# An FFT-like convolution kernel: v's row sums and differences move from GpSimd to VectorE, three quarters of v's statistics go to ACT, and a packed 32x32 product becomes a full one

## The chip, the cores and the metric

The kernel runs on one core of one Trainium2 chip. The metric is the device time of one execution in microseconds (us), the median of three runs. The engines are TensorE (PE, with its weight loads PEld), VectorE (DVE), ScalarE (ACT), GpSimd (POOL) and SyncE (SP), which here only issues transfers. Each of them takes its own instructions in order and waits for others by semaphores.

## The reference, cut to what matters

Sixteen images of sixteen channels, 256x256, float32, go through two layers with a skip connection each. The first is a group norm and a 3x3 circular convolution (written with FFTs). The second is a group norm and a Laplace neural operator: a forward transform, a mixing of channels per frequency (the steady part x1), and a sum of damped exponentials (the transient part x2).

```python
def _L1_conv_ref(x, ty, tx, weights_pole1, weights_pole2, weights_residue):
    ...
    alpha = jnp.fft.fft2(x, axes=(-2, -1))
    ...
    output_residue1 = jnp.einsum('biox,oxik->bkox', alpha, S)
    ...
    output_residue2 = jnp.einsum('bikpq,ikpq->bkpq', D, weights_residue)
    x1 = jnp.fft.ifft2(output_residue1, s=(Ny, Nx), axes=(-2, -1)).real
    ...
    E1 = jnp.exp(weights_pole1[..., None] * tyc)
    E2 = jnp.exp(weights_pole2[..., None] * txc)
    F = jnp.einsum('kbpq,bipz->kbiqz', output_residue2, E1)
    x2 = jnp.einsum('kbiqz,biqx->kizx', F, E2).real
    return x1 + x2 / Nx / Ny

# --- layer 0 (conv_preact) ---
x = x + _L0_conv_ref(_gn(x), L0_conv_weight)
# --- layer 1 (conv_preact) ---
x = x + _L1_conv_ref(_gn(x), L1_conv_ty, L1_conv_tx, ...)
```

Below, v is the result of the first layer. The group norm of the second needs v's mean and variance per group, and the transforms need the sums and differences of rows y and 255 - y of v.

## The kernel before

Everything is float32. There are four stretches in time: the convolution with v's statistics (during which small tables for the operator are also set up), the forward transforms, the mixing, and the inverse transforms with the output.

In the first stretch, `conv(g)` is one step of 387; 24 steps make one image. Each step issues sixteen small products on 32x32 tiles of TensorE. Every six steps, four 128x512 blocks of v (r = 0 to 3) are complete: two (r = 0, 1) belong to rows from the top, two (r = 2, 3), three steps later, to the mirrored rows.

```python
    vp = p1.enter_context(tc.tile_pool(name="vt", bufs=4))
    fp = p1.enter_context(tc.tile_pool(name="v_sums", bufs=2))
    ...
    vst = tp.tile([P, B, 8, 6], FP, name="vst", tag="vst")
    sums = tp.tile([P, 2, B, 8], FP, name="sums", tag="sums")
    ...
        for r in (0, 1) if g % 6 == 5 else (2, 3) if g % 6 == 2 else ():
            ...
            nc.scalar.activation(vt, acc[r], AF.Identity, bias=ready[b][1], **by_sums)
            if r % 2:
                nc.scalar.activation(
                    acc[r], vt, AF.Square, bias=shift[:, b : b + 1], accum_out=sums[:, 1, b, col]
                )
            else:
                later.append((g + 2, vst[:, b, col.start], vt))
            if r == 3:
                lo, hi = acc["v", 0], acc["v", 1]
                both = fp.tile([P, 2, 2, N], FP, name="vsum", tag="vsum")
                nc.gpsimd.tensor_tensor(both, lo, hi, ALU.add)
                nc.gpsimd.tensor_tensor(lo, lo, hi, ALU.subtract)
                folded.append((g + 3, b, u, (both, lo)))
        while later and (later[0][0] <= g or g >= 24 * B + 2):
            _, to, vt = later.pop(0)
            nc.vector.bn_stats(to, vt)
```

So ACT evicts all four blocks from PSUM; for two of them it also sums v and its square (the square goes to PSUM, over the block it came from). VectorE takes statistics of the other two. POOL makes the sum and the difference of the two halves, 128x1024 each, which go to HBM.

The statistics of an image of x come from VectorE and pass through TensorE (`ps_stat`, products with a single column) before its convolution can begin: sixteen `bn_stats`, a `bn_aggr` 24 steps ahead of the image, then operations on one column of `xq`, and the weights `wc`.

```python
        yield 24, lambda: nc.vector.bn_aggr(q[:, 0:2], st)
        ...
        yield 22, lambda: ps.append(spread(g128, mean))
        def about_mean():
            nc.vector.tensor_copy(mu, ps[0])
            nc.vector.tensor_tensor(d, mean, mu, ALU.subtract)
            nc.vector.scalar_tensor_tensor(e, d, d, pvar, ALU.mult, ALU.add)
        yield 21, about_mean
        yield 18, lambda: ps.append(spread(g128, e))
```

The table setup (`make_hat`, `make_c`, `make_exps`, `make_coef`) is spread over the same steps; it uses all engines, POOL among them. `make_exps` writes the exponentials to HBM:

```python
            nc.gpsimd.tensor_scalar(rn, th, 1.0 / (2 * PI), turns, ALU.mult, ALU.add)
            ...
            for c in (c1, c2, c3):
                nc.vector.scalar_tensor_tensor(th, rn, -float(c), th, ALU.mult, ALU.add)
            ...
            for o in range(2 - which):
                nc.sync.dma_start(
                    out=eD[which][o, :, 2 * q : 2 * q + 2].rearrange("p i e t -> p i (e t)"),
                    in_=ex,
                )
```

In the last stretch a unit is four images of one output channel k; there are 64. Per image there are four 128x128 products along x (`ps_p`), and four 128x256 products along y (`ps_f`), two for the steady part and two for the transient part. The transient factor along x (`ps_h`) is made for four images at once from 32x32 tiles:

```python
    def transient_x(k, b0):
        ps_h = [pf.tile([P, 2, N], FP, name="ps_h", tag="ps_f")[:, 0] for _ in range(4)]
        for j in range(4):
            for kq in range(4):
                rows = slice(32 * kq, 32 * kq + 32)
                c = 32 * ((kq + j) % 4)
                nc.tensor.matmul(
                    ps_h[j][c : c + 32],
                    lhsT=o2[rows, b0 + j].rearrange("p r m -> p (r m)"),
                    rhs=et[rows, k].rearrange("p e t -> p (e t)"),
                    start=True,
                    stop=True,
                )
        hs = hsp.tile([P, 4, N], FP, name="hs", tag="hs")
        for j in range(4):
            nc.scalar.copy(hs[:, j], ps_h[j])
        return hs
    ...
    def along_y(ey, hs, pt, r):
        ps = pf.tile([P, 2, N], FP, name="ps_f", tag="ps_f")
        for e, tab in ((0, cosY), (1, sinY)):
            nc.tensor.matmul(ps[:, e], lhsT=tab, rhs=pt[:, e], start=True, stop=False)
            nc.tensor.matmul(ps[:, e], lhsT=ey[:, e], rhs=hs, start=False, stop=True)
        ...
    def load_tables(k, eng=nc.gpsimd):
        eng.dma_start(out=et[:, k], in_=eD[1][0, :, k])
        ey = eyp.tile([P, 4, 2, P], FP, name="ey", tag="ey")
        for j in range(4):
            eng.dma_start(out=ey[:, j], in_=turned[P - 32 * j : 2 * P - 32 * j, k])
        return ey
```

Because the four tiles of image j land in output rows turned by 32 j, the table along y is loaded four times, turned likewise. A product written once in float32 shows as two instructions in the trace.

Of the kernel before, what the change touches and what calls it, by code (L numbers as in the profile page):

```python
# [16 lines left out]
B = 16  # L17
C = 16
# [6 lines left out]
def conv_then_laplace_kernel(ctx: ExitStack, tc: tile.TileContext, a: dict, out: bass.AP):  # L25
# [37 lines left out]
    eD = [dp.tile([n, P, C, 2, P], FP, name=f"eD{n}", tag=f"eD{n}") for n in (2, 1)]  # L63
# [37 lines left out]
    fp = p1.enter_context(tc.tile_pool(name="v_sums", bufs=2))  # L101
    sp = p1.enter_context(tc.tile_pool(name="stats", bufs=2))
# [110 lines left out]
    vst = tp.tile([P, B, 8, 6], FP, name="vst", tag="vst")  # L213
    sums = tp.tile([P, 2, B, 8], FP, name="sums", tag="sums")
    shift = tp.tile([P, B], FP, name="shift", tag="shift")

    def conv(g):
# [20 lines left out]
        for r in (0, 1) if g % 6 == 5 else (2, 3) if g % 6 == 2 else ():  # L238
            at = g if r < 2 else g - 3
            if not 0 <= at < 24 * B:  # L240
                continue
            b, u = at // 24, at // 6 % 4
            if r % 2 == 0:
                acc["v", r // 2] = vp.tile([P, 2, 2, N], FP, name="vt", tag="vt")
            vt = acc["v", r // 2][:, r % 2]
            col = slice(2 * u + r // 2, 2 * u + r // 2 + 1)
            by_sums = {"accum_out": sums[:, 0, b, col]} if r % 2 else {}
            nc.scalar.activation(vt, acc[r], AF.Identity, bias=ready[b][1], **by_sums)  # L248
            if r % 2:
                nc.scalar.activation(  # L250
                    acc[r], vt, AF.Square, bias=shift[:, b : b + 1], accum_out=sums[:, 1, b, col]
                )
            else:
                later.append((g + 2, vst[:, b, col.start], vt))
            if r == 3:
                lo, hi = acc["v", 0], acc["v", 1]
                both = fp.tile([P, 2, 2, N], FP, name="vsum", tag="vsum")
                nc.gpsimd.tensor_tensor(both, lo, hi, ALU.add)  # L258
                nc.gpsimd.tensor_tensor(lo, lo, hi, ALU.subtract)
                folded.append((g + 3, b, u, (both, lo)))  # L260
        while later and (later[0][0] <= g or g >= 24 * B + 2):
            _, to, vt = later.pop(0)
            nc.vector.bn_stats(to, vt)
# [16 lines left out]
    def v_stats(b0, b1, bank):  # L280

        bs, nb = slice(b0, b1), b1 - b0
        n = 8.0 * 512
# [13 lines left out]
        tt(mean, m1, m2, ALU.add)  # L297
        ts(mean, mean, 0.5, None, ALU.mult)
        tt(e, v1, v2, ALU.add)
# [5 lines left out]
        for m in (m1, m2):  # L305
            tt(d, m, mu, ALU.subtract)
            tt(d, d, d, ALU.mult)
            tt(e, e, d, ALU.add)
        ts(e, e, 0.5, None, ALU.mult)
# [86 lines left out]
    def make_coef():  # L396
# [3 lines left out]
        nc.sync.dma_start(out=rs, in_=a["res_kq"])  # L400
        u = sw.tile([P, 4, C, 4], FP, name="s_u", tag="s_rn")
# [15 lines left out]
    def make_exps(which):  # L417
# [10 lines left out]
        for q in range(8):  # L428
# [28 lines left out]
            for o in range(2 - which):  # L457
                nc.sync.dma_start(
                    out=eD[which][o, :, 2 * q : 2 * q + 2].rearrange("p i e t -> p i (e t)"),
                    in_=ex,  # L460
                )
# [583 lines left out]
    eyp = pool(p3, "ey", 2)  # L1045
    kp = pool(p3, "e_const")
    up = pool(p3, "ud", 2)
    hp = pool(p3, "pl", 3)
    hsp = pool(p3, "hl", 2)
    qp = pool(p3, "ql", 3)  # L1050
    pp = pool(p3, "p_p", 2, space=PSUM)
    pf = pool(p3, "p_f", 6, space=PSUM)

    et = ep.tile([P, C, 2, P], FP, name="et", tag="et")
    turned = eD[0].rearrange("o p k e t -> (o p) k e t")
    inv = kp.tile([P, 5, P], FP, name="inv", tag="inv")
    nc.gpsimd.dma_start(out=inv, in_=a["inv"])
    cx, sx, nsx, cosY, sinY = (inv[:, j] for j in range(5))
# [11 lines left out]
    def load_tables(k, eng=nc.gpsimd):  # L1070

        eng.dma_start(out=et[:, k], in_=eD[1][0, :, k])
        ey = eyp.tile([P, 4, 2, P], FP, name="ey", tag="ey")
        for j in range(4):
            eng.dma_start(out=ey[:, j], in_=turned[P - 32 * j : 2 * P - 32 * j, k])
        return ey
# [36 lines left out]
    def transient_x(k, b0):  # L1113


        ps_h = [pf.tile([P, 2, N], FP, name="ps_h", tag="ps_f")[:, 0] for _ in range(4)]
        for j in range(4):
            for kq in range(4):
                rows = slice(32 * kq, 32 * kq + 32)
                c = 32 * ((kq + j) % 4)  # L1120
                nc.tensor.matmul(  # L1121
                    ps_h[j][c : c + 32],
                    lhsT=o2[rows, b0 + j].rearrange("p r m -> p (r m)"),
                    rhs=et[rows, k].rearrange("p e t -> p (e t)"),
                    start=True,
                    stop=True,
                )
        hs = hsp.tile([P, 4, N], FP, name="hs", tag="hs")
        for j in range(4):
            nc.scalar.copy(hs[:, j], ps_h[j])  # L1130
        return hs

    def along_x(u):

        ps = pp.tile([P, 4, P], FP, name="ps_p", tag="ps_p")
        for n, (at, tab) in enumerate(((0, cx), (3, sx), (1, nsx), (2, cx))):
            nc.tensor.matmul(ps[:, at], lhsT=u[:, n], rhs=tab, start=True, stop=True)  # L1137
        pt = hp.tile([P, 2, N], FP, name="pt", tag="pt")
        nc.scalar.copy(pt, ps.rearrange("p (e n) x -> p e (n x)", e=2))
        return pt  # L1140

    def along_y(ey, hs, pt, r):

        ps = pf.tile([P, 2, N], FP, name="ps_f", tag="ps_f")
        for e, tab in ((0, cosY), (1, sinY)):
            nc.tensor.matmul(ps[:, e], lhsT=tab, rhs=pt[:, e], start=True, stop=False)  # L1146
            nc.tensor.matmul(ps[:, e], lhsT=ey[:, e], rhs=hs, start=False, stop=True)  # L1147
# [20 lines left out]
    ey = load_tables(0)  # L1168
# [3 lines left out]
    for b0 in range(4, B, 4):  # L1172
        load_images(yk, b0, slice(0, P), nc.sync)
# [190 lines left out]
```

## Time and profile before

The time is 2940.07 us, the median of three runs (2932.43, 2940.07 and 2942.22). The profiled execution has a span of 2938.3 us.

| engine | busy us | share of the span | instructions |
|---|---|---|---|
| PE | 2685.4 | 91% | 39536 |
| PEld | 1975.1 | 67% | 39536 |
| DVE | 1922.6 | 65% | 3508 |
| ACT | 1506.2 | 51% | 2955 |
| POOL | 1228.4 | 42% | 970 |

The costliest groups of instructions that the change touches or neighbours:

| group | count | busy us | mean ns |
|---|---|---|---|
| PE ps_conv, 32x512 on 32x32 tiles | 12288 | 493.7 | 649 |
| ACT vt, eviction of v, 128x512 | 256 | 161.4 | 681 |
| ACT square, 128x512 | 128 | 88.5 | 692 |
| ACT read of the accumulator after the square | 128 | 23.9 | 186 |
| ACT read of the accumulator after the eviction | 128 | 25.8 | 201 |
| DVE statistics of v, 128x512 | 128 | 86.6 | 677 |
| DVE statistics of x, 128x512 | 256 | 161.7 | 678 |
| PE ps_h, 32x256 on 32x32 tiles | 2048 | 59.5 | 385 |
| PE ps_f, 128x256, the two lines | 2048 | 610.6 | 380 |
| PE ps_p, 128x128 | 2048 | 278.1 | 279 |

"Busy" counts the time in which an engine has an instruction under way; matmuls are pipelined, their modelled durations overlap, and a busy TensorE need not be at its peak. Shares over the whole span mix four stretches with different limits, so each part of the change has to be read in its own stretch. A wait is named by the engine and line that ended it.

### The profile page before, as it was taken

What the parts mean: (1) busy time and instruction counts of PE and PEld (TensorE: products, weight loads), DVE (VectorE), ACT (ScalarE), POOL (GpSimd) and SP (SyncE); (2) the same over time, 40 slices, a digit from 0 to 9 for tenths busy, and PEclk for the clock granted to TensorE, in tenths of its full rate; (3) what the DMA queues carried; (4) which work ended last, traced back from release to release, by engine and by line L of the source; (5) the groups of instructions that cost most, each with busy time, mean ns of one, the idle gap of its engine ahead of it and who ended that gap; (6) DMA issues with size and microseconds to landing.
All of it is one profiled execution on the core that took longest, in us unless ns stands there. A gap on an engine that the chain in (4) does not pass through costs nothing.

```text
span 2938.3 us, 92782 instructions
## 1 busy us (share of the span) xinstructions
PE 2685.4 (91%) x39536; PEld 1975.1 (67%) x39536; DVE 1922.6 (65%) x3508; ACT 1506.2 (51%) x2955; POOL 1228.4 (42%) x970
## 2 busy tenths in 40 slices
PE   4878887777799999999699999999979999999998
PEld 2323333334577777777488888888868888888887
DVE  7666676887488888888544444444426676666666
ACT  3445566755566666666245555555534444444443
POOL 3656666775533333333311111111125555545543
PEclk9989988998899999999899999999989999999999
DMA  6545556674546666665466666667679898989895
GB/s 253 207 159 196 202 207 216 223 244 168 195 173 215 215 230 229 229 218 188 165 194 192 190 194 194 190 192 196 193 196 314 285 291 282 293 281 287 286 287 187
DMA packets 477332, 650.61 MB, mean 221 GB/s; under 512 B 49064, under 2 KB 458664, under 8 KB 462968
## 3 DMA queue, kind: packets, MB, share of 16 engines
q1 hardware_dynamic: 472920, 635.37, 66.7%
q8 instruction: 312, 5.11, 0.7%
q10 hardware_dynamic: 3408, 7.34, 0.7%
q0 software_dynamic: 592, 1.97, 0.3%
q14 instruction: 100, 0.82, 0.1%
HBM read 365.09 MB, written 279.45 MB: 219 GB/s over the span
## 4 chain that ended last, share of the span: by engine, by line
PE 54%; DMA 9%; DVE 7%; SPq 2%; issue 1%; POOL 1%; ACT 0%; DVEq 0%; ACTq 0%; POOLq 0%
PE ps_mix L956 15%; PE ps_s L898 8%; PE ps_y L667 8%; PE ps_y L675 7%; DMA yk<-yD 6%; PE ps_x L710 4%; PE ps_p L1137 3%; PE ps_f L1146 3%; PE ps_f L1147 3%; DVE r L1155 2%; DMA out_y<-ol 2%; SPq L1088 1%; PE psd L695 1%; DVE ol L1157 1%; DVE ol L1158 1%; PE ps_h L1121 1%
## 5 line engine op out<-in xcount | busy, mean ns | idle before, releaser
L231 PE MATMUL ps_conv<-xt,wc 32*32 32x512 f32 x12288 | 493.7, 649 | 30.4 <-ACT vt L248 20.3
L1101 POOL TENSOR_TENSOR u<-yk 128x512 f32<-128x512 f32 x256 | 343.9, 1373 | 369.0 <-PE ps_p L1137 252.6
L956 PEld LDWEIGHTS ps_mix<-abd,sg 128*64 128x64 f32 x8192 | 449.5, 138 | 61.5 <-ACT sg L1016 49.8
L956 PE MATMUL ps_mix<-abd,sg 128*64 128x128 f32 x8192 | 480.4, 276 | 9.5 <-ACT yt L1021 9.5
L231 PEld LDWEIGHTS ps_conv<-xt,wc 32*32 32x32 f32 x12288 | 234.0, 107 | 246.0 <-issue 151.6
L683 ACT ACTIVATE t<-ps_y,vmr 128x384 f32<-128x384 f32 x512 | 297.2, 581 | 170.4 <-PE ps_y L675 157.4
L876 POOL TENSOR_TENSOR w<-v,mcol 128x2048 f32<-128x2048 f32 x33 | 119.2, 3614 | 577.3 <-DVE v L873 574.3
L667 PE MATMUL ps_y<-tabE,vq 128*128 128x256 f32 x1024 | 313.0, 387 | 14.9 <-DVE vq L656 13.2
L1021 DVE COPY yt<-ps_mix 128x512 f32<-128x512 f32 x128 | 88.5, 692 | 360.9 <-PE ps_mix L956 225.2
L675 PE MATMUL ps_y<-tabO,vq 128*128 128x256 f32 x1024 | 305.7, 380 | 0.0
L1146 PE MATMUL ps_f<-pt,inv 128*128 128x256 f32 x1024 | 305.7, 380 | 0.0
L1147 PE MATMUL ps_f<-hs,ey 128*128 128x256 f32 x1024 | 304.9, 379 | 0.0
L1137 PEld LDWEIGHTS ps_p<-inv,u 128*128 128x128 f32 x2048 | 265.1, 192 | 49.1 <-issue 25.1
L1021 ACT COPY yt<-ps_mix 128x512 f32<-128x512 f32 x384 | 218.9, 587 | 149.6 <-PE ps_mix L956 86.5
L248 ACT ACTIVATE vt<-ps_conv,xq 128x512 f32<-128x512 f32 x256 | 161.4, 681 | 258.2 <-PE ps_conv L231 141.9
L1137 PE MATMUL ps_p<-inv,u 128*128 128x128 f32 x2048 | 278.1, 279 | 12.6 <-POOL u L1104 12.6
L898 PE MATMUL ps_s<-ct,w 64*32 64x256 f32 x8448 | 262.6, 384 | 18.6 <-POOL w L876 17.9
L1150 DVE TENSOR_TENSOR r<-ps_f,q 128x256 f32<-128x256 f32 x256 | 107.3, 419 | 252.9 <-ACT q L1149 252.9
L1016 ACT COPY sg<-ps_s 128x512 f32<-128x512 f32 x248 | 159.8, 646 | 197.4 <-PE ps_s L898 197.3
L667 PEld LDWEIGHTS ps_y<-tabE,vq 128*128 128x128 f32 x1024 | 189.4, 190 | 91.4 <-ACT q L723 51.2
L1149 ACT COPY q<-ps_f 128x256 f32<-128x256 f32 x256 | 95.3, 372 | 288.5 <-PE ps_f L1147 286.6
L258 POOL TENSOR_TENSOR vsum<-vt 128x1024 f32<-128x1024 f32 x64 | 153.0, 2391 | 194.1 <-ACT vt L248 119.9
(212 smaller groups left out, 4324.5 us busy)
## 6 DMA issues: line engine op xcount, KB each, us to landing
xt<-in_x SPq DMA_DIRECT2D x32, 2322.0 KB, 9.8
abd<-aD SPq DMA_DIRECT2D x512, 128.0 KB, 3.5
yD<-yt SPq DMA_DIRECT2D x512, 128.0 KB, 2.7
vl<-vD SPq DMA_DIRECT2D x256, 256.0 KB, 3.9
out_y<-ol SPq DMA_DIRECT2D x128, 512.0 KB, 9.6
yk<-yD SPq DMA_DIRECT2D x63, 1024.0 KB, 8.6
s<-vD SPq DMA_DIRECT2D x244, 256.0 KB, 6.7
aD<-spec SPq DMA_DIRECT2D x15, 4096.0 KB, 12.4
```

Of the source, the lines that this page charges most:

```text
L231: nc.tensor.matmul(acc[r][32 * c : 32 * c + 32], lhsT=ready[b][0][rows, phase, tap], rhs=halves[b][u // 2][rows, q : q + 5 : 4, 2 - tap : ...
L248: nc.scalar.activation(vt, acc[r], AF.Identity, bias=ready[b][1], **by_sums)
L667: nc.tensor.matmul(ps[:, 0:N], lhsT=vf[:, xo, 0, j], rhs=tabE[:, 0 : i + 2 : i + 1], start=True, stop=False, skip_group_check=True,)
L675: nc.tensor.matmul(ps[:, P : P + N], lhsT=vf[:, xo, 1, j], rhs=tabO[:, i : C + 1 : C - i], start=False, stop=True, skip_group_check=True,)
L683: nc.scalar.activation(t[:, xo, j].rearrange("p l n -> p (l n)"), ps[:, 0:384], AF.Copy, scale=vmr[:, 0, b0 + j, i : i + 1],)
L898: nc.tensor.matmul(ps[odd][32 * iq : 32 * iq + 32, ro], lhsT=w[rows, iq, kk, ro], rhs=ct[rows, iq, kk], start=True, stop=True,)
L956: nc.tensor.matmul(ps[64 * t : 64 * t + 64, j], lhsT=sg[:, f : f + 2].rearrange("p f m -> p (f m)"), rhs=abd[jq][:, :, 2 * t + cc, 2 * jj ...
L1021: (nc.vector.tensor_copy if m == 3 else nc.scalar.copy)(o, src)
L1101: nc.gpsimd.tensor_tensor(u[:, :, j].rearrange("p b (c n) -> p c b n", c=8), in0, in1, o)
L1137: nc.tensor.matmul(ps[:, at], lhsT=u[:, n], rhs=tab, start=True, stop=True)
L1146: nc.tensor.matmul(ps[:, e], lhsT=tab, rhs=pt[:, e], start=True, stop=False)
L1147: nc.tensor.matmul(ps[:, e], lhsT=ey[:, e], rhs=hs, start=False, stop=True)
```

## The change

It does two things. In the first stretch, the sum and the difference of v's halves are made by VectorE, two steps after the eviction, and POOL keeps only table setup. In return VectorE takes statistics of one block in four instead of two; ACT sums three, and writes the squares to a scratch tile in SBUF instead of PSUM. This is for taking the 128x1024 operations from the slower engine. In the last stretch, the packed 32x32 product of the transient factor is replaced by one full product per image: `ob` holds o2 times a block mask, made once, so that the blocks off the diagonal are zero; the tables need no turned copies then. PSUM is divided anew there (3, 2 and 3 buffers instead of 2 and 6). The formulas that combine the two kinds of statistics get the weights 1 and 3, and two more empty steps stand ahead of `make_coef`.

```diff
+    def mirror(g, b, u, lo, hi):
+        both = fp.tile([P, 2, 2, N], FP, name="vsum", tag="vsum")
+        nc.vector.tensor_tensor(both, lo, hi, ALU.add)
+        nc.vector.tensor_tensor(lo, lo, hi, ALU.subtract)
+        folded.append((g + 3, b, u, (both, lo)))
...
-            nc.scalar.activation(vt, acc[r], AF.Identity, bias=ready[b][1], **by_sums)
-            if r % 2:
+            col = slice(3 * u + r - 1, 3 * u + r)
+            by_sums = {"accum_out": sums[:, 0, b, col]} if r else {}
+            nc.scalar.activation(vt[:, r % 2], acc[r], AF.Identity, bias=ready[b][1], **by_sums)
+            if r == 0:
+                later.append((g + 2, lambda b=b, u=u, v=vt[:, 0]: nc.vector.bn_stats(vst[:, b, u], v)))
+            if r % 2 == 0:
+                continue
+            for k in (1,) if r == 1 else (2, 3):
+                col = slice(3 * u + k - 1, 3 * u + k)
+                junk = jp.tile([P, 2, N], FP, name="junk", tag="junk")
                 nc.scalar.activation(
-                    acc[r], vt, AF.Square, bias=shift[:, b : b + 1], accum_out=sums[:, 1, b, col]
+                    junk,
+                    vt[:, k % 2],
+                    AF.Square,
+                    bias=shift[:, b : b + 1],
+                    accum_out=sums[:, 1, b, col],
                 )
-            else:
-                later.append((g + 2, vst[:, b, col.start], vt))
             if r == 3:
-                lo, hi = acc["v", 0], acc["v", 1]
-                both = fp.tile([P, 2, 2, N], FP, name="vsum", tag="vsum")
-                nc.gpsimd.tensor_tensor(both, lo, hi, ALU.add)
-                nc.gpsimd.tensor_tensor(lo, lo, hi, ALU.subtract)
-                folded.append((g + 3, b, u, (both, lo)))
+                later.append((g + 2, lambda g=g, b=b, u=u, lo=acc["v", 0], hi=vt: mirror(g, b, u, lo, hi)))
...
-            for o in range(2 - which):
-                nc.sync.dma_start(
-                    out=eD[which][o, :, 2 * q : 2 * q + 2].rearrange("p i e t -> p i (e t)"),
-                    in_=ex,
-                )
+            nc.sync.dma_start(
+                out=eD[which][:, 2 * q : 2 * q + 2].rearrange("p i e t -> p i (e t)"), in_=ex
+            )
...
-    pp = pool(p3, "p_p", 2, space=PSUM)
-    pf = pool(p3, "p_f", 6, space=PSUM)
+    pp = pool(p3, "p_p", 3, space=PSUM)
+    ph = pool(p3, "p_h", 2, space=PSUM)
+    pf = pool(p3, "p_f", 3, space=PSUM)
...
+    ob = kp.tile([P, B, 2, 64], FP, name="ob", tag="ob")
+    for kq in range(4):
+        nc.vector.tensor_scalar(
+            ob[:, :, :, 16 * kq : 16 * kq + 16], o2, cols[:, 20 + kq : 21 + kq], None, ALU.mult
+        )
...
-        eng.dma_start(out=et[:, k], in_=eD[1][0, :, k])
-        ey = eyp.tile([P, 4, 2, P], FP, name="ey", tag="ey")
-        for j in range(4):
-            eng.dma_start(out=ey[:, j], in_=turned[P - 32 * j : 2 * P - 32 * j, k])
-        return ey
+        for j in (1, 0):
+            eng.dma_start(out=et[:, j, k], in_=eD[j, :, k])
...
-    def transient_x(k, b0):
...
+    def along_x(k, b, u):
+
+        ps_h = ph.tile([P, N], FP, name="ps_h", tag="ps_h")
+        nc.tensor.matmul(
+            ps_h,
+            lhsT=ob[:, b].rearrange("p r m -> p (r m)"),
+            rhs=et[:, 1, k].rearrange("p e t -> p (e t)"),
+            start=True,
+            stop=True,
+        )
```

## The prediction

> **What bounds the kernel now.** I read the page first (engines, slices, costliest groups), then the busy times of four stretches, because the page's shares average over stages with different limits. Columns: length, busy time with instruction count for TensorE (PE), its weight loads (PEld), VectorE (DVE), ScalarE (ACT) and GpSimd (POOL), then granted clock, DMA share, GB/s. The stretches are the convolution with v's statistics, the forward transforms, the mixing, and the inverse transforms with the output.
>
> ```profile
> 0.00:780.00 780.00, 597.04 (x12644) 283.68 (x12644) 530.43 (x841) 424.71 (x882) 486.48 (x320) 0.91 0.59 206
> 780.00:1410.00 630.00, 617.15 (x4100) 443.63 (x4100) 528.16 (x1213) 372.30 (x641) 220.53 (x285) 0.99 0.60 214
> 1410.00:2172.00 762.00, 731.45 (x16680) 610.99 (x16680) 357.89 (x751) 387.00 (x668) 140.80 (x46) 0.98 0.66 188
> 2172.00:2939.00 767.00, 739.76 (x6112) 636.80 (x6112) 506.14 (x704) 322.19 (x764) 380.62 (x320) 0.99 0.87 276
> ```
>
> Three stretches have TensorE busy 96 to 98% at almost full clock. The first is different: nothing is above 77% (TensorE, and that at a mean clock of 0.91), VectorE 68%, POOL 62%, ACT 54%. The change touches the first and the fourth.
>
> For the fourth I read its TensorE timeline. Columns: start, duration, engine, line, operation, tiles, count.
>
> ```profile
> 2518.86 0.59 PE L1147 MATMUL ps_f<-hs,ey 128*128 128x256 f32 x2
> 2519.38 0.81 PE L1121 MATMUL ps_h<-et,o 32*32 32x256 f32 x32
> 2520.13 1.16 PE L1137 MATMUL ps_p<-inv,u 128*128 128x128 f32 x8
> 2521.12 0.60 PE L1146 MATMUL ps_f<-pt,inv 128*128 128x256 f32 x2
> 2521.55 0.59 PE L1147 MATMUL ps_f<-hs,ey 128*128 128x256 f32 x2
> 2521.99 0.59 PE L1146 MATMUL ps_f<-pt,inv 128*128 128x256 f32 x2
> 2522.42 0.59 PE L1147 MATMUL ps_f<-hs,ey 128*128 128x256 f32 x2
> 2522.85 1.05 PE L1137 MATMUL ps_p<-inv,u 128*128 128x128 f32 x8
> ...
> 2530.80 0.81 PE L1121 MATMUL ps_h<-et,o 32*32 32x256 f32 x32
> ```
>
> Durations overlap, so starts are what to read. One full 128x256 product (two instructions) costs 21.99 - 21.55 = 0.43 us. Between the second and third products along x (2522.85 and 2525.47) an image takes 2.62 us. A unit of four images begins at each ps_h group: 2530.80 - 2519.38 = 11.42 us, of which the packed ps_h group is 11.42 - 4 x 2.62 = 0.94 us. One unit in four is longer, about 12.26 us, as the starts of all 64 groups show; the mean of 62 units after the start is 11.62, so the packed group costs 1.14 us a unit on average. TensorE follows itself without a gap here: the stage is bound by it, not by its 0.87 DMA share.
>
> For the first stretch I read the groups and the waits. Group columns: what it is, count | busy, mean ns | idle before it and who ended it. Wait columns: who waited for whom, total, times, longest.
>
> ```profile
> L259 POOL TENSOR_TENSOR vt<-vt 128x1024 f32<-128x1024 f32 x64 | 154.0, 2407 | 35.2 <-DVE vst L263 15.7 <-issue 15.0 <-DVE xq L174 0.2
> L258 POOL TENSOR_TENSOR vsum<-vt 128x1024 f32<-128x1024 f32 x64 | 153.0, 2391 | 194.1 <-ACT vt L248 119.9 <-DVE vst L263 61.2 <-DVE vs L304 7.3
> L445 DVE SCALAR_TENSOR_TENSOR s_th<-s_rn,s_th 128x512 f32<-128x512 f32 x48 | 73.7, 1535 | 10.6 <-POOL s_rn L439 9.5
> L143 DVE TENSOR_TENSOR xq<-xq 128x1 f32<-128x1 f32 x16 | 17.2, 1075 | 0.6
> PEld ps_stat L166 <- DVE xq L162: 74.5, 15, 10.5
> DVE vst L263 <- ACT vt L248: 85.9, 33, 6.3
> DVE xq L162 <- ACT vt L248: 55.3, 10, 13.5
> ACT vt L248 <- POOL s_th L434: 10.5, 3, 4.4
> ```
>
> The stage is a ring of in-order engines: ACT waits for the convolution, VectorE for ACT's v, TensorE for VectorE's image statistics. No engine is full; each is late at times. The last rows of the groups show something worth more than its size: a VectorE operation on one column takes 1075 ns. Its own listing gives a minimum of 159 ns, and for the 128x512 one (mean 1535) a minimum of 628. They sit through a POOL operation of 2.4 us.
>
> **What the Trainium skill says.** "SBUF — State Buffer", Who interferes with whom: a VectorE instruction with two SBUF inputs and a GpSimd instruction that reads SBUF exclude each other for a whole instruction. The minima and means above agree. "GPSIMD Engine Reference", Engine selection: an elementwise operation of two inputs is about twice as slow on GpSimd. The trace agrees: 2391 to 2407 ns for 128x1024, against 1219 ns for a VectorE tensor_tensor of that shape in the second stretch (L659). "TensorEngine Tiling (Array Packing)", Theoretical Speedup: 32x32 tiles give up to 16x. Here four images' factors cost 1.14 us instead of 4 x 0.43 = 1.73, so far less; the timeline shows thirty-two short instructions for it, and a slower first product after it (0.99 us to the next start instead of 0.89). "TensorE: Matmul & The Clock Gate", HAM oscillation: a TensorE idle for some microseconds starts again at half clock. The first stretch agrees: after the weight loads waited 8.55 us at 343 us, two groups of 32 weight loads start 1.71 us apart (344.78 and 346.49), where an unthrottled stretch has 0.87 (482.28 to 483.16).
>
> **The change, part by part.**
>
> 1. Stage four, transient factor along x. Removed: 32 packed instructions a unit, 1.14 us. Added: per image one full 128x128x256 product with the block-masked ob, 0.43 us, so 1.73 a unit. Net 0.59 x 64 = +37 us, all on the path. ACT's copies are the same in number; VectorE gets four 128x512 multiplications once (about 2 us, before TensorE has its first u at 2183). The tables fall from five 128 KB loads per k to two; 0.4 MB less x 16 = 6.3 MB, at 285 GB/s 22 us of DMA time, but hidden, since TensorE is what ends last. I count 0 for it.
>
> 2. Stage one, VectorE. Removed: 64 of 128 statistics at 677 ns, -43 us. Added: 128 sums and differences at 1.22 us, +156. Freed: for every VectorE group of the stage I took the sum of durations less its count times its minimum. That is 119 us, nearly all in two-input rows. POOL's busy time falls from 487 to about 180 (the table setup stays), so I let 45 of 119 remain, the new operations' own waits included: -74. Sum +39 us of VectorE work, from about 530 to 570; 73% of the stretch instead of 68.
>
> 3. Stage one, ACT. 64 more squares with their accumulator reads: 692 + 186 + 201 ns = 1.08 us each, +69 us, from 425 to 494. They come after the two evictions, so they delay only what follows them. The square now writes SBUF, so the PSUM bank is free after the eviction; waits for that square were 18.1 us on the weight-load side.
>
> 4. Stage one, POOL. 307 us off. ACT's waits on POOL (s_th 10.5 and 5.3, vsum 9.5, vt 7.1, s_rn 4.7 and 3.7, s_den 3.8: 44.6 us), TensorE's on POOL's s_num (13.8), ACT's on VectorE's slowed s_th (20.3) and the PSUM release (18.1) lose their cause: 97 us of waits. Engines alternate as the late one, so I count half, -49. Of the +39 on VectorE I also count about half, +20, since it idles 86 + 55 us waiting for ACT now. Net for stage one: -29 us, with an uncertainty of 45 either way, because halving is a choice and not a measurement.
>
> Sum: 2940 + 37 - 29 = 2948; with some room for small waits at the changes of stage I say 2950 us.
>
> **Rivals.** (a) VectorE becomes the bound of stage one. For it: several images already have VectorE without a gap before the aggregation (at 624 and 718 us TensorE waits 4.6 and 9.2 us for it), and TensorE can't go on without its statistics. Then all of +39, and the new operations waiting in order for ACT, count: stage one +40 to +60, total about 3020. Against it: 141 us of its idle time is waiting for ACT. (b) The lock was the disease: VectorE's chain of one-column operations, held up by POOL, starves TensorE, which then runs at half clock. Without it images would come every 42 us (the best now take 36, the mean is 46.5), stage one -70, total about 2907. For it: the clock of 0.91; against: the longest TensorE waits follow table setup and a DMA (s_kcol, 9.7 us), which stay. (c) Stage four is really fed by DMA, and lighter tables pay: +37 shrinks to about +15, total 2928. Against: the idle-free TensorE timeline.
>
> **Range and chances.** Part 1 is firm to some 6 us. The spread is stage one's, from -75 to +50, which gives 2895 to 3010. Faster by 2% is below 2881, which needs stage one to gain nearly 100: 0.10. Slower by 2% is above 2999, rival (a) in full: 0.13. Within: 0.77.
>
> **What would show it.** Unit starts in stage four 12.2 us apart, with ps_h at 0.43 us an image, no TensorE gaps and a DMA share near 0.83. In stage one: vsum on VectorE near 1.25 us, s_th near 0.8 us instead of 1.5, one-column operations near 0.3; VectorE busy near 570 and ACT near 494; POOL near 180; clock above 0.91; the stretch about 750 instead of 780. I am wrong if vsum averages much over 1.4 us (POOL's setup still locks it out), if TensorE's wait for L162's counterpart grows over 100 us, or if stage four's units aren't near 12.2.

## The result: 0.9% slower, and the profile after

| | median, us | runs, us |
|---|---|---|
| before | 2938.03 | 2932.43 to 2942.22 (4) |
| after | 2963.52 | 2960.16 to 2965.26 (4) |

The ratio is 1.0087, with a 95% interval of 1.0066 to 1.0108. The prediction was 2950 us, 2895 to 3010: the time is in the range, 13.5 us above the 2950. Where the time went is read from when each stage's first instruction starts in the two profiled executions:

| event | before, us | after, us | after minus before |
|---|---|---|---|
| last product of the convolution starts | 771.4 | 748.1 | -23.3 |
| first product of the transforms (`ps_y`) | 785.2 | 760.9 | -24.3 |
| first product of the mixing (`ps_mix`) | 1455.2 | 1438.3 | -16.9 |
| first product along x (`ps_p`) | 2183.0 | 2169.0 | -14.0 |
| end | 2938.3 | 2963.5 | +25.2 |

So there are three movements and not two: the first stage gained 24 us, the last lost 39 (from -14.0 to +25.2), and between them 7 us were given back at the change from the transforms to the mixing (and 3 more up to the last stage).

The busy times by stretch after, cut at its own stage borders (columns as in the prediction: length, busy times of PE, PEld, DVE, ACT, POOL, then clock, DMA share, GB/s):

```profile
0.00:756.00 756.00, 585.86 (x12644) 277.23 (x12644) 548.35 (x905) 474.80 (x1074) 205.42 (x192) 0.92 0.59 210
756.00:1386.00 630.00, 617.50 (x4100) 443.94 (x4100) 528.20 (x1213) 372.28 (x641) 220.22 (x284) 0.99 0.59 207
1386.00:2155.00 769.00, 726.33 (x16638) 607.56 (x16640) 358.66 (x754) 388.23 (x664) 139.25 (x43) 0.97 0.66 191
2155.00:2963.00 808.00, 785.16 (x4622) 717.91 (x4618) 513.68 (x705) 340.48 (x769) 388.06 (x320) 0.99 0.80 255
```

The last row is 97% TensorE (96% before), on a stretch that is longer by some 40 us; its DMA share has fallen from 0.87 to 0.80. TensorE's timeline there after (start, duration, engine, line, operation, tiles, count):

```profile
2502.34 0.59 PE L1126 MATMUL ps_h<-et,ob 128*128 128x256 f32 x2
2502.78 1.05 PE L1135 MATMUL ps_p<-inv,u 128*128 128x128 f32 x8
2503.67 0.60 PE L1146 MATMUL ps_f<-pt,inv 128*128 128x256 f32 x2
2504.10 0.59 PE L1147 MATMUL ps_f<-hs,et 128*128 128x256 f32 x2
2504.53 0.59 PE L1146 MATMUL ps_f<-pt,inv 128*128 128x256 f32 x2
2504.97 0.59 PE L1147 MATMUL ps_f<-hs,et 128*128 128x256 f32 x2
2505.40 0.59 PE L1126 MATMUL ps_h<-et,ob 128*128 128x256 f32 x2
...
2514.55 0.59 PE L1126 MATMUL ps_h<-et,ob 128*128 128x256 f32 x2
```

An image takes 2505.40 - 2502.34 = 3.06 us and a unit of four 2514.55 - 2502.34 = 12.21 us, with nothing between the products. The full product takes 2502.78 - 2502.34 = 0.44 us.

In the first stretch, the groups after, from 30 to 760 us (count | busy, mean ns | idle before, and who ended it) and then the waits after, from 30 to 770 us:

```profile
L221 DVE TENSOR_TENSOR vt<-vt 128x1024 f32<-128x1024 f32 x64 | 86.8, 1356 | 2.2
L220 DVE TENSOR_TENSOR vsum<-vt 128x1024 f32<-128x1024 f32 x64 | 80.0, 1250 | 63.5 <-ACT vt L255 63.5
L457 DVE SCALAR_TENSOR_TENSOR s_th<-s_rn,s_th 128x512 f32<-128x512 f32 x48 | 33.7, 703 | 1.1
L263 ACT ACTIVATE junk<-vt,shift 128x512 f32<-128x512 f32 x192 | 138.2, 720 | 4.2
L145 DVE TENSOR_TENSOR xq<-xq 128x1 f32<-128x1 f32 x15 | 7.5, 497 | 0.5
L144 DVE TENSOR_TENSOR xq<-xq 128x1 f32<-128x1 f32 x15 | 2.9, 190 | 0.5
```

```profile
ACT vt L255 <- PE ps_conv L238: 202.2, 72, 10.8
PEld ps_stat L167 <- DVE xq L163: 73.5, 15, 8.2
DVE vsum L220 <- ACT vt L255: 63.5, 25, 5.4
PEld ps_setup L552 <- POOL s_num L543: 1.6, 1, 1.6
```

`s_th` on VectorE went from 1535 to 703 ns, and the one-column operations of lines 143 and 144 of before (now 144 and 145), over the same 30 to 760 us, from 1136 and 875 to 190 and 497. TensorE's weight loads waited 17.5 us for POOL's `s_num` before and wait 1.6 us now. But the wait of TensorE for an image's aggregation is what it was: 73.5 us against 74.5. ACT, for its part, now waits longer for the convolution itself, 202.2 us against 141.4.

### The profile page after: what moved, and what is told of

It reads as the page before. It is cut to its first block, busy times and chain, and to the rows that moved or that the text cites. A ratio compares the mean times of both kernels' runs of the same rounds, so it can differ in the third digit from the quotient of the medians.

```text
span 2963.5 us, 89950 instructions
## 1 busy us (share of the span) xinstructions
PE 2714.8 (92%) x38000; PEld 2046.6 (69%) x38000; DVE 1948.9 (66%) x3576; ACT 1575.8 (53%) x3147; POOL 952.9 (32%) x839
## 5 line engine op out<-in xcount | busy, mean ns | idle before, releaser
L238 PE MATMUL ps_conv<-xt,wc 32*32 32x512 f32 x12288 | 480.5, 642 | 24.6 <-ACT vt L255 18.1
L1111 POOL TENSOR_TENSOR u<-yk 128x512 f32<-128x512 f32 x256 | 353.4, 1412 | 401.5 <-PE ps_p L1135 304.1
L238 PEld LDWEIGHTS ps_conv<-xt,wc 32*32 32x32 f32 x12288 | 227.1, 107 | 236.2 <-issue 149.0
L677 PE MATMUL ps_y<-tabE,vq 128*128 128x256 f32 x1024 | 313.2, 388 | 13.9 <-DVE vq L666 12.2
L1147 PE MATMUL ps_f<-hs,et 128*128 128x256 f32 x1024 | 304.8, 379 | 0.0
L1135 PE MATMUL ps_p<-inv,u 128*128 128x128 f32 x2048 | 271.7, 276 | 12.7 <-POOL u L1114 12.7
L255 ACT ACTIVATE vt<-ps_conv,xq 128x512 f32<-128x512 f32 x256 | 167.1, 681 | 202.9 <-PE ps_conv L238 202.2
L1139 ACT COPY pt<-ps_p 128x512 f32<-128x512 f32 x256 | 149.9, 585 | 147.0 <-PE ps_p L1135 147.0
```

Of the source, the lines that this page charges most:

```text
L238: nc.tensor.matmul(acc[r][32 * c : 32 * c + 32], lhsT=ready[b][0][rows, phase, tap], rhs=halves[b][u // 2][rows, q : q + 5 : 4, 2 - tap : ...
L255: nc.scalar.activation(vt[:, r % 2], acc[r], AF.Identity, bias=ready[b][1], **by_sums)
L677: nc.tensor.matmul(ps[:, 0:N], lhsT=vf[:, xo, 0, j], rhs=tabE[:, 0 : i + 2 : i + 1], start=True, stop=False, skip_group_check=True,)
L1111: nc.gpsimd.tensor_tensor(u[:, :, j].rearrange("p b (c n) -> p c b n", c=8), in0, in1, o)
L1147: nc.tensor.matmul(ps[:, e], lhsT=et[:, 0, k, e], rhs=hs, start=False, stop=True)
```

## The experiments

My theory at the start: the first part gains some 25 us since POOL no longer stands in VectorE's and the setup's way, the last part loses 37 to 39, and the 7 us between come from neither, but from where a buffer lies in SBUF. Each part was run alone first. Times of one group of experiments are compared with runs of the kernel before that were made beside them (2935.97 us for e1 to e4, 2937.13 for e5 to e8, 2939.45 for e9 and e10, 2938.91 for e11 and e12). Unless it says otherwise, each computes all that the kernel before computes. "Delay" means an event's start in the profile less the same event's before.

### e1: the first part alone

Edit: all hunks of the change in the first stretch but the exponentials' stores, on the kernel before; the packed product stays.

> The kernel before with the first stretch's change alone (sums and differences on VectorE, three quarters of v's statistics on ACT); the last stretch keeps the packed product. Parts add (mine): the convolution ends about 23 us earlier, 7 us of it are lost again at the change to the mixing stretch, so about 2921 us. Rival, that the first stretch's gain came from the lighter exponential tables of the last stretch's change: no gain, about 2938.

Measured: 2923.53 us, ratio 0.9935 (0.991 to 0.996). The convolution's last product is at -29.8, the first `ps_y` at -31.1, the first `ps_mix` at -22.9, the end at -27. So the first part gains, and gives 8 us back at the mixing here too.

### e2: the last part alone

Edit: the hunks of the last stretch alone, with the exponentials' stores that belong to them (these run in the first stretch).

```diff
-    pp = pool(p3, "p_p", 2, space=PSUM)
-    pf = pool(p3, "p_f", 6, space=PSUM)
+    pp = pool(p3, "p_p", 3, space=PSUM)
+    ph = pool(p3, "p_h", 2, space=PSUM)
+    pf = pool(p3, "p_f", 3, space=PSUM)
...
+        ps_h = ph.tile([P, N], FP, name="ps_h", tag="ps_h")
+        nc.tensor.matmul(ps_h, lhsT=ob[:, b]..., rhs=et[:, 1, k]..., start=True, stop=True)
```

> The kernel before with the last stretch's change alone (one full product per image instead of packed tiles). Parts add (mine): 64 units at 12.2 us instead of 11.6, +37 to +40 us, about 2977. Rival, that the last stretch is fed by DMA and only started earlier or later because of the first: under +15, about 2950. The convolution's end should not move by more than 3 us.

Measured: 2981.88 us, ratio 1.0151 (1.0132 to 1.0171), +46. From the first to the last `ps_p` the delay grows from +4.8 to +43.6: the last stretch costs 39 us. The convolution ended 5.8 us late in this profile, where I had allowed 3, though only the exponentials' stores had changed beside it; runs of the kernel before spread over 15 us (2930.6 to 2946.1), so a few us in one profile say nothing.

### e3: the changed kernel with 1 KB of padding in SBUF

The table pool of the first stretch holds `vst` and `sums`, whose sizes the change alters: `vst` from 3072 to 1536 bytes a partition, `sums` from 1024 to 1536. Whatever is placed later can move by 1 KB. The edit gives that space back, by a tile that nothing uses:

```diff
     shift = tp.tile([P, B], FP, name="shift", tag="shift")
+    tp.tile([P, 256], FP, name="pad", tag="pad")
```

> The changed kernel with an unused tile of 1 KB per partition in the pool of tables, which gives the later pools their old places. If the 7 us lost at the change to the mixing stretch come from the place of ct, which now overlaps the last spectrum buffer and waits until that has been stored (mine): ct is issued before the forward transforms end, about 2956 us. If they come from the order in which work arrives: ct still waits for the store, 2963.

Measured: 2953.25 us, ratio 1.0051 (1.0032 to 1.007). The delay at the first `ps_y` is -27.3 and at the first `ps_mix` -28.4: nothing is given back. What happened at that border shows in the view of one tile, `ct`, a table that is loaded before the mixing (duration in ns, then start of its issue in us). Before, after, and e3:

```profile
L828 SPq DMA_DIRECT2D ct<-cD x1: 365/365/365, 1394.6 to 1394.6; - x1
```

```profile
L838 SPq DMA_DIRECT2D ct<-cD x1: 326/326/326, 1396.7 to 1396.7; - x1
```

```profile
L839 SPq DMA_DIRECT2D ct<-cD x1: 367/367/367, 1368.6 to 1368.6; - x1
```

And what TensorE's first `ps_s` products, which read `ct`, were idle for between 1370 and 1460 us, after and in e3 (last field: idle, and who ended it):

```profile
L908 PE MATMUL ps_s<-ct,w 64*32 64x256 f32 x824 | 27.8, 415 | 27.0 <-DMA ct<-cD 27.0
```

```profile
L909 PE MATMUL ps_s<-ct,w 64*32 64x256 f32 x960 | 32.7, 415 | 17.8 <-POOL w L887 17.6 <-issue 0.2
```

Before, the load was issued 10 us before the transforms' last product (1405 us). After, that product came 24 us earlier and the load 2 us later, so that TensorE stood for 27 us and until the load had landed. The transfer queue's own wait in after says for what, between 1300 and 1500 us:

```profile
SPq L838 <- DMA aD<-spec: 24.7, 1, 24.7
```

The load into `ct` waited for the store of the last spectra from SBUF to HBM. It has no data in common with it. With the padding the wait is gone from that line. That the two share SBUF space in after is inferred from the wait and its disappearance. That the placement costs 7 to 11 us is what the medians say, here (1.0087 against 1.0051) and in e1 against e5 (0.9935 against 0.9913), though the intervals of each pair just overlap. The stage says it more clearly: from the first `ps_y` to the first `ps_mix` it takes 677.4 us in the changed kernel and 678.2 in e1, which have the new sizes without padding, and 668.3 to 670.7 in the kernel before and all the other runs.

### e4: sums and differences on VectorE alone

Edit: the statistics stay as before, half on VectorE and half on ACT.

```diff
-                nc.gpsimd.tensor_tensor(both, lo, hi, ALU.add)
-                nc.gpsimd.tensor_tensor(lo, lo, hi, ALU.subtract)
+        nc.vector.tensor_tensor(both, lo, hi, ALU.add)
+        nc.vector.tensor_tensor(lo, lo, hi, ALU.subtract)
```

> The kernel before with the sums and differences on VectorE, but statistics as before (half on VectorE, the square over its PSUM bank). If POOL's two-input operations were what held VectorE up (mine): most of the gain is here, the convolution ends 5 to 20 us before the kernel before's 771, about 2925 us, with s_th near 0.7 us. If the gain needs ACT to take statistics, because VectorE is full: the convolution ends at 771 or later, 2940 to 2960.

Measured: 2917.1 us, ratio 0.9936 (0.9913 to 0.9958). VectorE's busy time in the first 780 us:

```profile
0.00:780.00 780.00, 604.35 (x12670) 288.16 (x12671) 598.59 (x992) 428.78 (x888) 209.18 (x196) 0.90 0.60 212
```

VectorE is at 599 of 780 us, and the kernel is still faster: VectorE is not the bound (rival (a) falls), and most of the gain is in this half of the first part.

### e5: the first part alone, padded

Edit: e1 with e3's padding.

> The first stretch's change alone with the unused 1 KB tile, packed product kept. Mine: the run without the tile (2923) less the 7 to 10 us that the place of ct costs, about 2915, ct issued before the forward transforms end. Base of the next two runs. Rival: nothing but scatter, 2923.

Measured: 2911.65 us (2906.13 to 2916.96), ratio 0.9913 (0.989 to 0.9935). The convolution ends at -31.2, the first `ps_mix` is at -32.1. This is what the first part is worth: 25 us by the medians.

### e6: more statistics on ACT, sums and differences still on POOL

Edit: on e5, the two operations go back to POOL, at once and not two steps later.

```diff
-        nc.vector.tensor_tensor(both, lo, hi, ALU.add)
-        nc.vector.tensor_tensor(lo, lo, hi, ALU.subtract)
+        nc.gpsimd.tensor_tensor(both, lo, hi, ALU.add)
+        nc.gpsimd.tensor_tensor(lo, lo, hi, ALU.subtract)
```

> The kernel before with three quarters of v's statistics on ACT and squares to SBUF, padded likewise; sums and differences stay on POOL. If POOL was the cause of the gain (mine): VectorE loses 43 us of work but keeps its waits in POOL's operations, s_th stays near 1.5 us, so the convolution's end moves by less than 10 us, 2930 to 2940. If VectorE's load was what counted: -20 or more, 2915.

Measured: 2940.71 us (20 runs), ratio 1.0014 (1.0005 to 1.0024), a loss of 1.5 to 7 us. Windows of e6, and one row of its groups:

```profile
0.00:780.00 780.00, 593.66 (x12644) 283.82 (x12644) 480.23 (x779) 476.19 (x1074) 487.51 (x320) 0.90 0.59 207
```

```profile
L458 DVE SCALAR_TENSOR_TENSOR s_th<-s_rn,s_th 128x512 f32<-128x512 f32 x48 | 78.4, 1634 | 13.4 <-POOL s_rn L452 12.3
```

VectorE has 50 us less to do than before (480 against 530) and nothing comes of it, while POOL still stretches its two-input operations (1634 ns).

### e7 and e8: POOL busy again, once reading and once writing only

Both stand on e5 and add work on POOL that nothing uses, in each of the 64 groups, on the scratch tile `proj` (its shapes are left out in the diffs): e7 two additions that read v, about as long as those of before; e8 one small reading and five fillings, which write only.

```diff
+                for _ in range(2):
+                    nc.gpsimd.tensor_tensor(proj, vt, vt, ALU.add)          # e7
```

```diff
+                nc.gpsimd.tensor_scalar(proj[:, 0:1], vt[:, 1, 1, N-1:N], 0.0, None, ALU.mult)
+                for _ in range(5):
+                    nc.gpsimd.memset(proj, 0.0)                             # e8
```

> The first part padded (sums and differences on VectorE), and POOL does again two 128x1024 additions of two SBUF inputs after each pair of evictions, into a tile that nobody reads. If the mutual exclusion of such operations with VectorE's two-input ones was what the change removed (mine): s_th and the one-column operations get long again (1.0 to 1.5 us), vsum rises over 1.8 us, POOL's setup is late again, the gain is gone and more: 2945 to 2990. If only the wait for POOL's results mattered: no change from the base, about 2915.

> As the last, but POOL fills the unread tile five times (writes only, about the same 4.5 us of POOL time a group) after one small read. If exclusion at the reads is the cause (mine): VectorE's durations stay as in the base, only POOL's setup is late; at most +10 us over the base, 2915 to 2925. If POOL being occupied (late table setup) is the cause: as slow as with the additions.

Measured: e7 2982.34 us, ratio 1.015 (1.0127 to 1.0173), 71 us over e5. e8 2937.55 us, ratio 0.9997 (0.9984 to 1.001), 26 us over e5. The groups of e7, then of e8, in the first 760 us of each (a count under 64, 128 or 320 is what was done by then):

```profile
L273 POOL TENSOR_TENSOR proj<-vt 128x1024 f32<-128x1024 f32 x112 | 246.3, 2199 | 224.8 <-ACT vt L256 220.3
...
L222 DVE TENSOR_TENSOR vt<-vt 128x1024 f32<-128x1024 f32 x55 | 105.6, 1920 | 4.0 <-DVE vsum L221 0.5
L221 DVE TENSOR_TENSOR vsum<-vt 128x1024 f32<-128x1024 f32 x55 | 79.1, 1438 | 34.2 <-ACT vt L256 34.1
L465 DVE SCALAR_TENSOR_TENSOR s_th<-s_rn,s_th 128x512 f32<-128x512 f32 x48 | 61.3, 1278 | 9.0 <-POOL s_rn L459 8.0
```

```profile
L274 POOL MEMSET proj<- 128x1024 f32 x305 | 293.9, 964 | 17.6
...
L222 DVE TENSOR_TENSOR vt<-vt 128x1024 f32<-128x1024 f32 x61 | 82.2, 1347 | 4.6 <-POOL proj L274 0.5
L221 DVE TENSOR_TENSOR vsum<-vt 128x1024 f32<-128x1024 f32 x62 | 77.6, 1251 | 53.9 <-ACT vt L256 49.5 <-DMA vD<-vt 4.2
...
L461 DVE SCALAR_TENSOR_TENSOR s_th<-s_rn,s_th 128x512 f32<-128x512 f32 x48 | 35.0, 729 | 17.9 <-POOL s_rn L455 16.7
```

This is the rule that "SBUF — State Buffer", Who interferes with whom, of the Trainium skill gives: VectorE operations with two SBUF inputs exclude POOL operations that read SBUF, not those that only write it. The trace agrees: 294 us of filling leave `s_th` at 729 ns (703 without), 246 us of reading make it 1278. POOL is even busier in e8 than in e7 (542 against 468 us of the first 780), so mere occupation is not what makes e7 slower. Part of the 45 us between them shows in TensorE's wait for an image's statistics (30 to 770 us; e7, then e8):

```profile
PEld ps_stat L167 <- DVE xq L163: 93.0, 15, 15.6
```

```profile
PEld ps_stat L167 <- DVE xq L163: 67.9, 15, 7.7
```

TensorE's granted clock in the first 780 us is 0.88 in e7 and 0.91 in e8, so another part may pass through a slower TensorE; the runs do not part the two.

Three expectations were missed. In e7 I had `vsum` above 1.8 us; it took 1438 ns, and the difference after it 1920. I had the one-column operations at 1.0 to 1.5 us; those on `xq` with two inputs took 0.46 to 0.93 us. And e8 should have cost at most 10 us over e5 and cost 26: POOL is in the way even where it locks nothing. Its wait rows say how, but two causes are mixed there (e8, waits):

```profile
ACT vt L256 <- POOL proj L274: 34.8, 12, 5.9
PEld ps_setup L558 <- POOL s_num L549: 25.4, 5, 7.0
...
DVE s_th L461 <- POOL s_rn L455: 16.7, 6, 6.1
```

The first is a buffer of v that comes free late, as the small reading queues behind fillings. The others are the table setup, whose POOL steps queue there too.

### e9 and e10: a wait of the ring that neither kernel cures

TensorE's wait of 74 us for an image's aggregation stayed. VectorE's `bn_aggr` waits in turn for ACT's eviction (55 us before, 44 after), though it needs nothing from it: the tile `xq` holds the bias that ACT's evictions read, it has two buffers, and the aggregation writes the one of the image two back. The edit gives it a pool with three, on e5 (e9) and on the kernel before (e10).

```diff
+    sq = p1.enter_context(tc.tile_pool(name="stats_q", bufs=3))
...
-        q = sp.tile([P, 12], FP, name="xq", tag="xq")
+        q = sq.tile([P, 12], FP, name="xq", tag="xq")
```

> The first part alone with the padding, and a third buffer for the 128x12 tile of the columns of an image of x (xq), so that bn_aggr of an image no longer waits until ACT's last eviction of the image two before has read its bias. In e5 VectorE still idles 44 us in the stretch at L163 waiting for ACT, and TensorE's weight loads wait about 71 us for the columns. My theory: this ring wait is real path in part; VectorE's wait for ACT at bn_aggr falls below 10 us, the weight loads' wait for xq falls to 40 to 60 us, and the time falls by 5 to 20 us against e5, to about 2892 to 2907 (ratio to before 0.985 to 0.990). Rival: the aggregation is never what ends the wait, because the sixteen statistics of x ahead of it keep VectorE late anyway; the wait moves to the next line and the time stays within 4 us of e5 (2908 to 2916).

> The kernel before with the same third buffer for xq and nothing else. There VectorE idles 55 us at L162 for ACT. If that wait was a separate disease of the ring, curable without moving any work, the time falls by 5 to 20 us here too (2918 to 2933). If in the kernel before the POOL operations set the pace (they hold VectorE's columns up and fill POOL's queue), it stays within 4 us of before.

Measured: e9 2904.34 us, ratio 0.988 (0.9864 to 0.9896); e10 2927.17 us, ratio 0.9953 (0.994 to 0.9967). The aggregation in e9 and TensorE's wait for it (groups, then waits):

```profile
L164 DVE BATCH_NORM_AGGREGATE xq<-xst 128x2 f32<-128x96 f32 x16 | 9.3, 584 | 0.4
```

```profile
PEld ps_stat L168 <- DVE xq L164: 54.2, 12, 8.3
```

VectorE's idle time there fell from 43 to 0.4 us, TensorE's wait from 71 (e5) to 54. The gain is 12 us on the kernel before and 7 on e5 by the medians (10 by the ratios; the intervals of e5 and e9 just overlap). It is a fault of its own, which needs no work moved. e9 is the fastest version found, 35 us under the kernel before and 59 under the changed one.

### e11 and e12: the same without v's buffers

These were to part the two causes in e8, and to show whether e7 lost its time by the mutual exclusion or by v's buffers. POOL waits for a column of the sums instead of v, so that no buffer of v depends on it; e11 has five fillings as e8, e12 two additions on `proj` itself (which it also clears once, at the start).

```diff
+                nc.gpsimd.tensor_scalar(proj[:, 0:1], sums[:, 1, b, col], 0.0, None, ALU.mult)
+                for _ in range(5):
+                    nc.gpsimd.memset(proj, 0.0)                             # e11
+                for _ in range(2):
+                    nc.gpsimd.tensor_tensor(proj, proj, proj, ALU.add)      # e12, instead
```

> As e8 (the first part alone with the padding, and five memsets of 128x1024 per group on POOL), but the small operation that paces them reads a column of the sums instead of v's buffer, so that no buffer of v waits for POOL. In e8 the evictions of v waited 34.8 us for that operation, because it queued behind memsets. If e8's 26 us over e5 came from buffers of v that came free late, most of it goes away here: 2908 to 2920. My theory: most of it is the table setup that queues behind POOL's work in order (TensorE's setup products waited 25.4 us for POOL in e8), so the time stays at 2928 to 2942; VectorE's durations as in e5 in both.

> As e7 (two POOL additions of 128x1024 per group), but on a tile of POOL's own instead of v, paced by a column of the sums; no buffer of v waits for POOL. POOL is occupied about as long as in e11, and it reads two SBUF inputs, which e11 does not. If the readings themselves hold VectorE up (mutual exclusion), e12 is 30 to 55 us above e11, at 2960 to 2985, with s_th over 1.2 us and vsum over 1.4 us. Rival: in e7 the time was lost since v's buffers came free late; then e12 is within 15 us of e11, whatever its VectorE durations are.

Measured: e11 2951.15 us, ratio 1.0042 (1.0027 to 1.0057); e12 2993.22 us, ratio 1.0199 (1.0164 to 1.0234). Two rows of e11's waits, then rows of e12's groups:

```profile
PEld ps_setup L558 <- POOL s_num L549: 34.0, 5, 8.3
...
DVE s_th L461 <- POOL s_rn L455: 21.4, 6, 6.4
```

```profile
L275 POOL TENSOR_TENSOR proj<-proj 128x1024 f32<-128x1024 f32 x108 | 224.5, 2079 | 8.7
L223 DVE TENSOR_TENSOR vt<-vt 128x1024 f32<-128x1024 f32 x54 | 84.8, 1571 | 1.9
...
L462 DVE SCALAR_TENSOR_TENSOR s_th<-s_rn,s_th 128x512 f32<-128x512 f32 x48 | 60.7, 1264 | 16.1 <-POOL s_rn L456 15.0
```

With v's buffers free of POOL, e11 did not fall back to e5, but rose, to about 38 us over it by the ratios. So the loss does not need late buffers of v, and the waits that remain on POOL are nearly all the setup's: 34.0 us for `s_num`, 21.4 us for `s_rn`, where e5 has 1.8 us for `s_num` and none for `s_rn`. How much of e8's 26 us its late buffers made is not shown, because e11 moves the fillings too (they begin later, after ACT's last square); why it is 14 us slower than e8 stays open. Both absolute times are above what I expected, and e12's `vsum` took 1368 ns where I had over 1400. The difference was expected and came: e12 is 42 us above e11, as e7 is 45 above e8, though POOL's additions occupy it for less time than the fillings. The readings themselves cost 42 to 45 us.

## Why the prediction was right, point by point

**Part 1, the last stretch, +37.** It measured +39, in the changed kernel and in e2 alone: 0.44 us for a full product, 12.21 us a unit where 12.2 was expected, no gap. (The 21.99 - 21.55 of the working is 0.44; the neighbouring starts give its 0.43.) The old unit I had read only in part. I had TensorE without a gap there, but most of the first units of an output channel took 12.26 us and not 11.42, since the packed product shared `ps_f`'s PSUM buffers and waited for VectorE's reading of the last one (before, from 2183 us on):

```profile
PE ps_h L1121 <- DVE r L1151: 4.3, 13, 0.3
```

So the packed group itself is the 0.94 us, and the 1.14 is an average with that wait in it. The change has no such wait, with PSUM divided anew, and all units take 12.21 us. The average gave the right sum; what packing costs with another division of PSUM no run shows. Lighter tables paid nothing (rival (c)): 0.87 of DMA share became 0.80, a little less than the 0.83 I expected, and the unit is what TensorE's products add up to.

**Part 2, VectorE, +39 us of work.** The sum of durations in the stage rose by 20 us only, from 571 to 591 (busy 530 to 548, not 570). The new operations took 167 us and not 156, because the differences took 1356 ns instead of the 1.22 us of a row elsewhere; but about 103 us of the old operations' durations came free and not 74, most of it in `xq` (-41) and `s_th` (-40). I had counted 119 us of excess over the minima and let 45 remain for POOL's setup. Over all groups it was 134 and is 46 now; without the statistics, 116 and 32, the new operations' own included.

**Part 3, ACT, +69.** The durations of ACT's operations rose by 75 us (the squares to SBUF take 720 ns instead of 692), its busy time by 50 (425 to 475), since accumulator reads partly lie beside other operations. No time lost by it shows: e4, which leaves ACT as before, ends within 10 us of e1 and e5, and their intervals overlap.

**Part 4, POOL, and the halving.** The net for the stage was -29, "with an uncertainty of 45 either way, because halving is a choice and not a measurement". It measured -24 in the changed kernel (at the first `ps_y`), and the median of e5 puts it at -25. The experiments give the parts, in the order e6, e7, e8, e5:

| step | what changes | us |
|---|---|---|
| before to e6 | a quarter of the statistics from VectorE to ACT | +4 |
| e6 to e7 | 128 sums and differences put on VectorE, POOL as busy as before | +42 |
| e7 to e8 | POOL writes only instead of reading: the mutual exclusion goes | -45 |
| e8 to e5 | POOL free: the setup no longer queues behind it (v's late buffers of e8 are in here too) | -26 |

In my own terms the relief of POOL was the -49 of waits and half of the -74, -86 in all, and the added work on VectorE half of 156 - 43, +56. Measured are -71 and +46 (42 + 4), so each was too large, by 15 and 10 us with opposite signs, and the sum right: that it fits so well is in part luck, since nothing had measured the halves. The mechanism stands. Of the 97 us of waits that I had listed, the trace of after has 11 left (ACT's on POOL 0, TensorE's on `s_num` 0.7, ACT's on `s_th` 9.7, those for a square's PSUM bank 0.7). POOL's busy time in the stage is 205 us, not 180. The relief is two effects of a like order: VectorE not held up, which e7 against e8 and e12 against e11 show, and POOL's in-order queue not delaying its own setup steps, which is read from the waits of e8, e11 and e5. Another order of the steps may share the sum out differently; no run shows it.

**Rivals.** (a) VectorE as the bound is refuted by e4 and e6: 50 us less work on it gave nothing and 68 us more still left a gain. (b) The lock as the whole disease: images came every 44.9 us ((748.1 - 30.0) / 16; 46.4 before, likewise), not every 42. The lock was 42 to 45 us, but the work on VectorE took as much back. The clock's part is not settled. Over the stretch it went from 0.91 to 0.92 only, but half of the stage's gain falls between 40% and 50% of the convolution's products, and there it rose (that tenth before, then after):

```profile
370.10:450.00 79.90, 62.24 (x1296) 28.16 (x1297) 60.08 (x91) 51.65 (x109) 55.54 (x44) 0.86 0.61 212
```

```profile
370.70:437.00 66.30, 54.91 (x1307) 26.27 (x1290) 59.74 (x92) 56.46 (x129) 21.10 (x24) 0.95 0.69 244
```

The tenth is 13.6 us shorter. TensorE is busy 7.3 us less in it, for about as many instructions, at 0.95 instead of 0.86, and its wait for POOL's `s_num` fell from 6.0 to 0.7 us. So a shorter wait and a faster TensorE come together here, which is the second half of rival (b); the runs do not part them. In e7 and e12, where the stretch grew, the clock was 0.88.

**The missing term.** "Some room for small waits at the changes of stage" was 2 us and should have been 10: 7 us at the border of transforms and mixing, by the placement of `ct`, and 3 up to the last stage (for these no cause was found; from the first `ps_mix` to the first `ps_p` the runs scatter from 725 to 734 us). I had not compared where buffers lie, though two tile sizes in the change say that they move. That term, two us more in the last stretch and 5 less gain in the first stage are the 13.5 us between 2950 and 2963.5 (8 + 2 + 5 = 15, from single profiles).

**What stays open.** Why the first stage gains where it does: the delay is +0.6 us at 40% of the convolution's products, -13.0 half way, -14.4 at 80% and -23.4 at 90%. The setup of tables is spread over the stage, but no run moved that. And rival (c) was not tested by adding transfers; that lighter tables gain nothing rests on e2's +39 and the timeline.

## What to carry to other kernels

When two in-order engines stand in each other's way, count separately what the relief of one frees (its lock on the other, and its own queue's other duties) and what the added work on the other costs; here these were -71 and +46 us, and only the runs with filler work on POOL told them apart. A change of tile sizes in one stage can add a wait in another: if a stage border gives time back, look there for a load that waits for an unrelated store, and try padding. A buffer that holds a small value read late (a bias of 4 bytes a partition) can hold a ring to two images; one more buffer of 48 bytes gave 7 to 12 us.

## What the runs showed of the hardware that I had not expected

- POOL filling SBUF for 294 us leaves VectorE's two-input operations at their own speed (729 ns against 703), while 225 to 246 us of POOL reading takes them to 1264 and 1278 ns. That is the skill's rule; new to me is that POOL occupied without any lock cost 26 us (e8) and 38 (e11).
- The packed 32x32 product is worth keeping at 0.94 us a unit (1.14 with its waits) against 4 x 0.43: replacing it cost 39 us in 64 units.
- An ACT square of 128x512 into SBUF takes 720 ns, into PSUM 692.
- On VectorE the in-place difference of 128x1024 takes 1356 ns, the sum just ahead of it 1250; with POOL reading beside them 1920 and 1438 in e7, 1571 and 1368 in e12: the second of the pair was hit harder.
